# Attention in a fused layer: one exponential over four PSUM banks in place of two over two banks each

## The chip, the core and the metric

The kernel runs on one NeuronCore of a Trainium2 chip, as one program with one launch. The metric is the time of one execution in microseconds on the device. The kernel before takes 879.42 us, the median of 3 runs (879.39 to 880.23).

## What is computed

A transformer layer: grouped-query cross-attention on normalized rows, and then a feed-forward layer with 32 routed experts (8 chosen for each row) and a shared expert. The change lies in the attention.

```python
# x (16, 128, 512), ctx (16, 128, 128); 32 query heads of 16, 8 key/value heads
def attention(q, k, v):
    qh = q.reshape(B, S, KV, G, D).transpose(0, 2, 3, 1, 4)   # KV 8, G 4, D 16
    kh = k.reshape(B, S, KV, D).transpose(0, 2, 1, 3)
    vh = v.reshape(B, S, KV, D).transpose(0, 2, 1, 3)
    scores = einsum('bkgsd,bktd->bkgst', qh, kh) / sqrt(D)
    weights = softmax(scores, axis=-1)
    out = einsum('bkgst,bktd->bkgsd', weights, vh)
    return out.transpose(0, 3, 1, 2, 4).reshape(B, S, E)

x = x + attention(layernorm(x), ctx, ctx)
x = x + moe(layernorm(x))     # gate, 8 of 32 experts, a shared expert
```

## The kernel before

The work is in three stages: attention (up to about 103 us), an end of attention with the last gate logits, the routing and the shared expert (its last shared matmuls start at 210.7 us), and the routed experts (the rest). All engines but the DMA queues of SP run in an order that the source writes out by hand (`manual_schedule`): an engine works through its instructions in the order in which the code issues them, and waits where a semaphore has not come.

**The steps.** `attention_small` makes 32 steps, two for each of the 16 batch elements: in step n, `items[n]` is (b, i), and i picks every other key/value head. The loop at L650 issues, in step n and in this order:

- `head` work: masking of keys (`keys`, L373, on ScalarE, in steps 4, 5, 9, 11, 17 and 19), squares of keys (`squares`, L394, ScalarE, steps 21, 23, 25 and 27), and work for VectorE and GpSimd;
- `scores` of step n (L484): four matmuls (L489), one for each of four key/value heads, each on its own 32 rows of the array (a row tile), each to its own PSUM bank of 128 x 512 float32. Each float32 matmul stands in the trace as two passes, so a step has eight records. Then the exponentials on ScalarE (L499), which read PSUM and write the probabilities `p` to SBUF;
- `values` of step n-1 (L502): four matmuls (L505), which read the probabilities and write one bank, `oT`; VectorE copies it to SBUF as `oTs` (L514);
- in steps 16, 20, 24 and 28 (and 31, after the loop) `gate_parts` (L563), four matmuls (L566) and a copy by ScalarE (L575);
- `transposes` (L447) of one or two sets into the tile `x` of two banks: queries of a later step, normalized rows for the gate, and the attention output of step n-2. ScalarE copies queries as `qT` (L480) and rows as `xall` (L543); VectorE divides the output by the sums (L523, L525), and GpSimd adds it to `x` (L532);
- in steps 17, 21, 25 and 29 `gate_sums` (L577), and then `tail` work, mostly statistics on VectorE.

**PSUM.** There are eight banks. `ps_sc` has two buffers of two banks for the scores, `ps_x` one of two banks, `ps_lg` and `ps_oT` one bank each: eight in all. In `scores`, matmuls 0 and 1 go to the first tile of `ps_sc` and 2 and 3 to the second; each tile has its exponential. The next step's first pair waits for this step's first exponential, and its second pair for the second. The probabilities of a step lie in two tiles of `pp`, which has five buffers.

**The end of attention (L683 to L721).** The scores' banks are used again: `two`, a pair of banks for transposes, and `gu`, a pair for the gate and up sums of the shared expert. `filler(n)` issues the next n matmuls of the shared expert (L282) between other work: the first one after step 31's transposes, the second after the gate parts of rows 8 and 9. The turn of the rows of batch element 15 takes a new pair from `ps_sc` (L714). The last logits let routing begin on ScalarE (L1151) and VectorE (L1159).

Of the kernel before, what the change touches and what calls it, by code (L numbers as in the profile page):

```python
# [9 lines left out]
F32 = mybir.dt.float32  # L10
F16 = mybir.dt.float16
I32 = mybir.dt.int32
AF = mybir.ActivationFunctionType
ALU = mybir.AluOpType
AX = mybir.AxisListType
PSUM = bass.MemoryType.PSUM
DRAM = bass.MemoryType.DRAM

P = 128
EPS = 1e-5  # L20
HD = 16
# [25 lines left out]
def tile_xattn_moe(  # L47
# [15 lines left out]
    nc = tc.nc  # L63
    B, S, D = x.shape
    E, _, ND, I = w1.shape
# [4 lines left out]
    TB = 512  # L70
# [160 lines left out]
    def gate_rows(b, eng):  # L231
        xn = xnp.tile([P, D], F32, tag="xn2", name="xn2", bufs=4)
        normalized(xn, xs[b], b, SECOND, eng)
        nc.sync.dma_start(rows[ts(b, P), 0:D], xn)
        xn2[b] = xn
# [62 lines left out]
    NJ = KV // 2  # L298
    quarter = [slice(4 * k, 4 * k + 4) for k in range(NTB)]

    def attention_small():


        with ExitStack() as ph:
            kpool = ph.enter_context(tc.tile_pool(name="kp", bufs=1))
            ap2 = ph.enter_context(tc.tile_pool(name="ap2", bufs=2))
            pp = ph.enter_context(tc.tile_pool(name="pp", bufs=5))
            ps_sc = ph.enter_context(tc.tile_pool(name="ps_sc", bufs=2, space=PSUM))
            ps_x = ph.enter_context(tc.tile_pool(name="ps_x", bufs=1, space=PSUM))
            ps_lg = ph.enter_context(tc.tile_pool(name="ps_lg", bufs=1, space=PSUM))  # L310
            ps_oT = ph.enter_context(tc.tile_pool(name="ps_oT", bufs=1, space=PSUM))
            qTs, ps, oTs, xqs = {}, {}, {}, {}
# [127 lines left out]
            halves = [slice(h * H, (h + 1) * H) for h in range(2)]  # L440

            def bank_pair(pool):
                return pool.tile(
                    [P, 2, 2, 2, P], F32, tag=("x" if pool is ps_x else "sc"), name="x"
                )

            def transposes(*sets, x=None, between=()):  # L447

                x = bank_pair(ps_x) if x is None else x
                for s, (of, split, _) in enumerate(sets):  # L450
                    for k in range(4):
                        for h, rows in enumerate(halves):
                            if split:
                                to = x[:, h, :, s, ts(k, P // 4)]
                                by = ident[rows, rows].rearrange("p (a b) -> p a b", a=2)
                            else:
                                to = x[:, h, k // 2, s, ts(k % 2, H)]
                                by = ident[rows, rows]
                            nc.tensor.matmul(  # L459
                                to,  # L460
                                lhsT=of[rows, k, :],
                                rhs=by,
                                start=True,
                                stop=True,
                                is_transpose=True,
                                tile_position=(h * H, 0),
                            )
                for s, (_, _, then) in enumerate(sets):
                    if s == len(sets) - 1:
                        for f, a in between:  # L470
                            f(*a)
                    then(x[:, :, :, s])
# [9 lines left out]
                return xn, False, then  # L482

            def scores(b, i):  # L484
                scs = [ps_sc.tile([P, 2, TB], F32, tag="sc", name="sc") for _ in range(NJ // 2)]
                qT = qTs[b].rearrange("p h r s -> p (h r s)")
                for j in range(NJ):
                    rows = slice(j * HP, (j + 1) * HP)
                    nc.tensor.matmul(  # L489
                        scs[j // 2][:, j % 2],  # L490
                        lhsT=kzs[b // 4 % 2][rows, b % 4, i, :],
                        rhs=qT[rows],
                        start=True,
                        stop=True,
                        tile_position=(j * HP, 0),
                    )
                for j, sc in enumerate(scs):
                    p = pp.tile([P, 2, TB], F32, tag="p", name="p")
                    nc.scalar.activation(p, sc, AF.Exp, scale=1.0 / HD**0.5)  # L499
                    ps[b, i, 2 * j], ps[b, i, 2 * j + 1] = p[:, 0], p[:, 1]  # L500

            def values(b, i):  # L502
                oT = ps_oT.tile([P, TB], F32, tag="oT", name="oT")
# [37 lines left out]
            def turn_of(b, copy=nc.scalar.copy):  # L541
                def then(x):
                    copy(  # L543
                        xnT[b // 4][:, :, ts(b % 4, P)].rearrange(
                            "p (r k) (h s) -> p h r k s", r=2, h=2
                        ),
                        x.rearrange("p h r (k s) -> p h r k s", k=2),
                    )

                return xn2.pop(b).rearrange("p (k d) -> p k d", d=P), False, then  # L550
# [99 lines left out]
            for n in range(N):  # L650
                for f, a in head.get(n, ()):
                    f(*a)

                scores(*items[n])
                if n == 1:
                    transposes(queries(1))
                if n > 0:
                    values(*items[n - 1])
                if n in parts and n < N - 1:
                    gate_parts(parts[n])  # L660
                sets = []
                if n % 2 == 0 and 0 < n // 2 < B - 1:
                    sets.append(queries(n // 2 + 1))
                if n in turned:
                    sets.append(turn_of(turned[n]))
                if n > 1:
                    sets.append(added(*items[n - 2], nc.gpsimd if n < N - 1 else nc.vector))
                if n == N - 1:
                    sets.reverse()
                between = middle.get(n, ())  # L670
                if sets:
                    transposes(*sets, between=between)
                else:
                    assert not between
                keep_warm(FILL.get(n, 0))
                if n in sums:
                    gate_sums(sums[n])
                for f, a in tail.get(n, ()):
                    f(*a)
# [2 lines left out]

            gate_rows(12, nc.gpsimd)  # L683
            nc.scalar.activation(table, table, AF.Sigmoid)
            two = bank_pair(ps_sc)
            gu = ps_sc.tile([P, 2, TB], F32, tag="sc", name="gu")
            banks = iter([gu[:, i] for i in range(2)])
            later, products = [], []
            matmuls = shared_up(0, 0, lambda: next(banks), later, products)

# [20 lines left out]
            filler(1)  # L711
            gate_parts(12)
            gate_rows(15, nc.vector)
            transposes(turn_of(15), x=bank_pair(ps_sc))  # L714
            gate_rows(14, nc.vector)
            transposes(turn_of(14, nc.vector.tensor_copy))
            gate_sums(12, nc.scalar.copy)
# [1199 lines left out]

    pieces = [(k, i) for k in range(NTB) for i in range(NI)]
    left_over = attention_small()
    experts(pieces[1:], in_order, *left_over)  # L1920
    left = nc.values_load(
# [64 lines left out]
```

## Time and profile before

The profile is of one execution on the chip. Its own time is 881.58 us, its span (first to last instruction) 879.7 us; the median of the runs is 879.42 us.

| What | Value |
|---|---|
| time of the profiled execution / its span | 881.58 / 879.7 us |
| TensorE matmuls busy | 861.7 us (98% of the span) |
| ScalarE, VectorE, GpSimd busy | 689.4, 625.9, 476.4 us |
| exponentials (L499), 64 of 128 x 1024 | 62.1 us, 1023 ns each |
| score matmul records (L489), 256 | 44.2 us, 639 ns each |
| value matmul records (L505), 256 | 34.1 us, 605 ns each |
| ScalarE idle before exponentials, ended by scores | 13.6 us, 23 times |

A line of a timeline gives the start in us from the start of the span, the duration in us, the engine, the line of the source, the operation, output and input tiles with their shape, and how many instructions are merged in it; in brackets stands the idle time of the engine before it and what ended it. "PE" is TensorE's matmul and "PEld" its loading of weights, which can run beside it. Records of matmuls on different row tiles overlap, so busy time is not a measure of how full the array is. A line of a group gives its busy time and the mean of one instruction, and after the second bar the idle time before it and what ended that. The chain of waits follows the work that ended last back to what released it.

Busy time of the engines by stage (us; the steps' first half, second half, the end of attention, and the beginning of routing):

| Stretch | length | PE | DVE | ACT | POOL |
|---|---|---|---|---|---|
| 8.8 to 55.5 | 46.70 | 46.27 | 39.16 | 37.91 | 24.43 |
| 55.5 to 102.8 | 47.30 | 47.30 | 34.59 | 41.04 | 31.73 |
| 102.8 to 120.2 | 17.40 | 15.86 | 11.05 | 8.93 | 8.29 |
| 120.2 to 160.0 | 39.80 | 39.80 | 34.73 | 11.72 | 9.04 |

### The profile page before, as it was taken

How to read it: one execution, taken by the hardware profiler on the slowest of the kernel's cores; microseconds unless marked ns; L12 is line 12 of the kernel's file. 1: busy time of each engine (PE TensorE's matmuls, PEld its weight loads, DVE VectorE, ACT ScalarE, POOL GpSimd, SP SyncE). 2: the span in 40 equal slices, each digit the busy share in tenths (PEclk: the TensorE clock that was granted, in tenths of full speed). 3: DMA queues.
4: the chain of work that ended last, by engine and by line, in shares of the span. 5: the costliest groups of instructions: out<-in, count | busy, mean ns of one | idle time of the engine just before them, and what ended most of it. 6: DMA issues, size and time to landing. Idle time of an engine off the chain costs nothing.

```text
span 879.7 us, 13628 instructions
## 1 busy us (share of the span) xinstructions
PE 861.7 (98%) x4015; PEld 538.5 (61%) x4015; DVE 625.9 (71%) x1599; ACT 689.4 (78%) x1570; POOL 476.4 (54%) x590
## 2 busy tenths in 40 slices
PE   8999999999899999999999999999999999999995
PEld 5344444546565665666666666676767777777763
DVE  7877778846976777777777777776867777777510
ACT  5888732537998898888898989898898899999831
POOL 4487550053355576656556666565556656554454
PEclk9999999999999999999999999999999999999999
DMA  9111112556377788778778787877778888786544
GB/s 307 58 48 50 49 50 77 211 156 197 110 169 162 172 202 191 177 169 182 165 181 184 192 188 191 186 210 175 187 158 206 195 176 178 197 190 122 88 76 54
DMA packets 59876, 137.15 MB, mean 156 GB/s; under 512 B 12168, under 2 KB 16392, under 8 KB 59792
## 3 DMA queue, kind: packets, MB, share of 16 engines
q0 software_dynamic: 32032, 69.25, 41.9%
q1 hardware_dynamic: 27680, 66.81, 22.1%
q8 instruction: 34, 0.56, 0.3%
q14 instruction: 50, 0.41, 0.2%
q10 hardware_dynamic: 80, 0.13, 0.0%
HBM read 96.71 MB, written 46.73 MB: 163 GB/s over the span
## 4 chain that ended last, share of the span: by engine, by line
PE 88%; POOL 3%; ACT 3%; issue 2%; DVE 2%; DMA 2%; POOLq 0%; ACTq 0%
PE p L1612 42%; PE y L1749 24%; PE gu L282 6%; PE sc L489 5%; PE oT L505 4%; PE x L459 2%; PE y L1386 2%; POOL out_dram L1721 2%; ACT xall L1506 2%; DMA out_dram<-yw,token 1%; PE tok L1038 1%; DVE x L1396 1%; PE lgT L566 0%; PE lg L581 0%; DVE xall L1506 0%
## 5 line engine op out<-in xcount | busy, mean ns | idle before, releaser
L1506 ACT COPY xall<-blocks 32x256 f32<-32x256 f32 (+10 forms) x1137 | 418.9, 368 | 15.0
L1721 POOL DMA_INDIRECT out_dram<-yw,token x150 | 246.2, 1641 | 212.0 <-ACT yw L1765 79.7
L1749 PE MATMUL y<-wdn,sa 128*128 128x512 f32 (+2 forms) x672 | 259.1, 594 | 0.0
L1460 POOL DMA_INDIRECT xgs<-rows,token x138 | 150.7, 1092 | 134.5 <-DVE token L1050 53.2
L1612 PE MATMUL p<-xall,wup 128*128 128x270 f32 (+27 forms) x720 | 185.6, 394 | 2.0 <-ACT p L1661 2.0
L1612 PEld LDWEIGHTS p<-xall,wup 128*128 128x128 f32 x720 | 136.5, 190 | 46.6 <-issue 16.1
L1749 PEld LDWEIGHTS y<-wdn,sa 128*128 128x128 f32 (+2 forms) x672 | 100.9, 171 | 83.7 <-issue 72.2
L1765 ACT ACTIVATE yw<-y,wt 128x512 f32<-128x512 f32 x138 | 94.7, 686 | 70.6 <-PE y L1749 39.4
L1612 PE MATMUL p<-t,s 128*128 128x270 f32 (+27 forms) x480 | 125.7, 394 | 1.1 <-DVE t L1603 1.1
L1612 PEld LDWEIGHTS p<-t,s 128*128 128x128 f32 x480 | 91.0, 190 | 39.0 <-issue 22.4
L1509 DVE STREAM_TRANSPOSE blocks<-xgs 128x512 f32<-128x512 f32 x138 | 97.5, 706 | 0.2
L1622 DVE TENSOR_TENSOR z<-u,p 128x270 f32<-128x270 f32 (+27 forms) x96 | 48.8, 509 | 68.5 <-PE p L1612 63.3
L499 ACT ACTIVATE p<-sc 128x1024 f32<-128x1024 f32 x64 | 62.1, 1023 | 13.6 <-PE sc L489 13.6
L1612 PE MATMUL p<-t,wup 128*128 128x270 f32 (+27 forms) x240 | 63.8, 396 | 0.7 <-DVE z L1622 0.7
L1612 PE MATMUL p<-xall,s 128*128 128x270 f32 (+27 forms) x240 | 63.6, 396 | 0.5 <-DVE z L1622 0.4
L1612 PEld LDWEIGHTS p<-t,wup 128*128 128x128 f32 x240 | 45.0, 190 | 25.9 <-issue 14.1
L282 PE MATMUL gu<-xall,sup 128*128 128x512 f32 x128 | 59.2, 601 | 0.0
L1622 DVE TENSOR_TENSOR u<-u,p 128x270 f32<-128x270 f32 (+27 forms) x48 | 24.4, 509 | 44.9 <-PE p L1612 36.9
L1612 PEld LDWEIGHTS p<-xall,s 128*128 128x128 f32 x240 | 45.2, 190 | 16.9 <-issue 4.3
L1506 DVE COPY xall<-blocks 32x256 f32<-32x256 f32 (+11 forms) x187 | 51.3, 299 | 3.5
L489 PE MATMUL sc<-qT,kz 32*128 32x512 f32 x256 | 44.2, 639 | 0.5 <-DVE qT L480 0.2
L1603 DVE TENSOR_TENSOR t<-xall,t 128x540 f32<-128x540 f32 (+27 forms) x60 | 43.3, 722 | 0.5
(218 smaller groups left out, 916.2 us busy)
## 6 DMA issues: line engine op xcount, KB each, us to landing
wup<-in_w_dram SPq DMA_DIRECT2D x64, 512.0 KB
wdn<-in_w_dram SPq DMA_DIRECT2D x32, 512.0 KB
rows<-xn SPq DMA_DIRECT2D x16, 256.0 KB
out_dram<-x SPq DMA_DIRECT2D x16, 256.0 KB
x<-in_x_dram SPq DMA_DIRECT2D x15, 256.0 KB
out_dram<-yw,token POOLq DMA_INDIRECT x150
xgs<-rows,token POOLq DMA_INDIRECT x138
cTs<-in_cT_dram SPq DMA_DIRECT2D x4, 256.0 KB
```

Source lines behind the costliest of these rows:

```text
L282: nc.tensor.matmul(acc, lhsT=sup[:, w, d, ts(i, P)], rhs=xnT[k][:, d, :], start=(d == 0), stop=(d == ND - 1),)
L489: nc.tensor.matmul(scs[j // 2][:, j % 2], lhsT=kzs[b // 4 % 2][rows, b % 4, i, :], rhs=qT[rows], start=True, stop=True, tile_position=(j * ...
L499: nc.scalar.activation(p, sc, AF.Exp, scale=1.0 / HD**0.5)
L1460: nc.gpsimd.indirect_dma_start(out=t, out_offset=None, in_=rows[:, :], in_offset=bass.IndirectOffsetOnAxis(ap=token[:, j : j + 1], axis=0) ...
L1506: yield on_ACT, 1 + many, lambda dst=dst, of=of, copy=copy: copy(dst, of)
L1509: nc.vector.transpose(blocks[:, j % NB_BUF, :], xgs[:, j % NG_BUF, 0:D])
L1603: yield lambda o=out_, a=a, b=b: nc.vector.tensor_tensor(o, a, b, ALU.subtract)
L1612: nc.tensor.matmul(acc[:, i, 0:h], lhsT=w[:, i, d, :], rhs=x[:, d, :], start=(first and i == d == 0), stop=(i == outs[-1] and d == 1), ski ...
L1622: soon(lambda: nc.vector.tensor_tensor(out_, a, b, ALU.add))
L1721: ins = nc.gpsimd.indirect_dma_start(out=flat, out_offset=bass.IndirectOffsetOnAxis(ap=token2[:, k - 1 : k] if a else token[0:b, j : j + 1 ...
L1749: nc.tensor.matmul(y[c0:c1, :], lhsT=acts_of[k % NA][:, i, col : col + c1 - c0], rhs=wdn[k % NW][:, i, :], start=(i == 0), stop=(i == NI - 1),
L1765: nc.scalar.activation(yws[j], y, AF.Copy, scale=wt[:, j : j + 1])
```

## The change

The scores of a step go to one tile of four banks, and one exponential of 128 x 2048 reads it. `ps_sc` has one buffer of four banks in place of two of two, so PSUM holds the same eight banks. The probabilities of a step are one tile, and `pp` has three buffers of it in place of five half as large. At the end of attention one four-bank tile, `four`, stands for `two` and `gu`, and the turn of element 15 uses its first half again instead of taking a new pair. The matmuls, their order and all other work stay as they are. In the changed source the exponential stands at L496, the scores at L487, the values at L503 and the transposes at L457.

```diff
-            pp = ph.enter_context(tc.tile_pool(name="pp", bufs=5))
-            ps_sc = ph.enter_context(tc.tile_pool(name="ps_sc", bufs=2, space=PSUM))
+            pp = ph.enter_context(tc.tile_pool(name="pp", bufs=3))
+            ps_sc = ph.enter_context(tc.tile_pool(name="ps_sc", bufs=1, space=PSUM))
...
             def scores(b, i):
-                scs = [ps_sc.tile([P, 2, TB], F32, tag="sc", name="sc") for _ in range(NJ // 2)]
+                sc = ps_sc.tile([P, NJ, TB], F32, tag="sc", name="sc")
                 qT = qTs[b].rearrange("p h r s -> p (h r s)")
                 for j in range(NJ):
                     rows = slice(j * HP, (j + 1) * HP)
                     nc.tensor.matmul(
-                        scs[j // 2][:, j % 2],
+                        sc[:, j],
                         lhsT=kzs[b // 4 % 2][rows, b % 4, i, :],
                         rhs=qT[rows],
                         start=True,
                         stop=True,
                         tile_position=(j * HP, 0),
                     )
-                for j, sc in enumerate(scs):
-                    p = pp.tile([P, 2, TB], F32, tag="p", name="p")
-                    nc.scalar.activation(p, sc, AF.Exp, scale=1.0 / HD**0.5)
-                    ps[b, i, 2 * j], ps[b, i, 2 * j + 1] = p[:, 0], p[:, 1]
+                p = pp.tile([P, NJ, TB], F32, tag="p", name="p")
+                nc.scalar.activation(p, sc, AF.Exp, scale=1.0 / HD**0.5)
+                for j in range(NJ):
+                    ps[b, i, j] = p[:, j]
...
-            two = bank_pair(ps_sc)
-            gu = ps_sc.tile([P, 2, TB], F32, tag="sc", name="gu")
-            banks = iter([gu[:, i] for i in range(2)])
+            four = ps_sc.tile([P, NJ, TB], F32, tag="sc", name="four")
+            two = four[:, 0:2].rearrange("p h (r s t) -> p h r s t", r=2, s=2)
+            banks = iter([four[:, i] for i in (2, 3)])
...
-            transposes(turn_of(15), x=bank_pair(ps_sc))
+            transposes(turn_of(15), x=two)
```

More of the change, by code (lines that the diff above doesn't have):

```diff
@@ L442, in bank_pair @@
             def bank_pair(pool):
-                return pool.tile(
-                    [P, 2, 2, 2, P], F32, tag=("x" if pool is ps_x else "sc"), name="x"
-                )
+                return pool.tile([P, 2, 2, 2, P], F32, tag="x", name="x")
             def transposes(*sets, x=None, between=()):
```

## Prediction

> **What bounds the kernel now.** I read the page first: one core, granted clock at full speed in every slice, and a chain that is TensorE for 88% of the span. The lines of the changed code in it are the scores (L489), the values (L505) and the transposes (L459).
>
> ```profile
> PE 88%; POOL 3%; ACT 3%; issue 2%; DVE 2%; DMA 2%; POOLq 0%; ACTq 0%
> PE p L1612 42%; PE y L1749 24%; PE gu L282 6%; PE sc L489 5%; PE oT L505 4%; PE x L459 2%; PE y L1386 2%; POOL out_dram L1721 2%; ACT xall L1506 2%; DMA out_dram<-yw,token 1%; PE tok L1038 1%; DVE x L1396 1%; PE lgT L566 0%; PE lg L581 0%; DVE xall L1506 0%
> ```
>
> So only the first 103 us matter, where 32 attention steps run; the rest is downstream of them. The timeline of steps 18 and 19 shows the order on TensorE: scores, values of the step before, transposes, sometimes gate work, and the next scores.
>
> ```profile
> 62.38 1.14 PE L489 MATMUL sc<-qT,kz 32*128 32x512 f32 x8
> ...
> 63.45 1.06 PE L505 MATMUL oT<-p,va 128*32 128x512 f32 x8
> 63.62 1.94 ACT L499 ACTIVATE p<-sc 128x1024 f32<-128x1024 f32 x2 [0.85 <-PE sc L489]
> ...
> 64.45 0.46 PE L459 MATMUL x<-ident,xq 64*128 64x64 f32 x8
> ...
> 64.75 0.41 PE L459 MATMUL x<-ident,oTs 64*128 64x64 f32 x8
> 65.09 0.30 PEld L489 LDWEIGHTS sc<-qT,kz 32*128 32x128 f32 x4
> 65.09 1.65 PE L489 MATMUL sc<-qT,kz 32*128 32x512 f32 x8
> ...
> 65.61 0.30 PEld L489 LDWEIGHTS sc<-qT,kz 32*128 32x128 f32 x4 [0.22 <-ACT p L499]
> ...
> 66.67 1.06 PE L505 MATMUL oT<-p,va 128*32 128x512 f32 x8
> ```
>
> Read it as a loop of two engines. Undisturbed scores take TensorE 1.07 us (62.38 to 63.45), values 1.00 (to 64.45), two sets of transposes 0.64 (to 65.09): 2.71 us a step. The exponentials begin 1.24 after the scores' start (63.62) and end at 65.56, 3.18 after it. TensorE is back at 65.09, so step 19 starts its first pair on banks that the first exponential has freed, and its second pair at 65.61, 0.05 after the second exponential. TensorE therefore already waits for ScalarE in many steps, but only with half of its scores: those groups last up to 1.8 us instead of 1.07. Long and short steps alternate (2.71 from 62.38 to 65.09, then 3.22 to 68.31).
>
> **What the Trainium skill says.** (1) "ScalarE: Activation LUTs", *What ACT_TABLE_LOAD costs*: an ACTIVATE with immediate scale and bias takes 186 ns + 0.833 ns an element, and back-to-back ones overlap by about 93 ns. For 1024 elements that is an estimated 1.04 us; the trace has 1.02 (row below), and two take 1.94, an overlap of 0.10. It agrees.
>
> ```profile
> L499 ACT ACTIVATE p<-sc 128x1024 f32<-128x1024 f32 x64 | 62.1, 1023 | 13.6 <-PE sc L489 13.6
> ```
>
> (2) "TensorEngine Tiling (Array Packing)", *Key Properties*: different tiles work in parallel. The trace agrees: four row tiles with two passes each end in 1.07 us, though one pass alone reads 0.6. Hence a late pair costs its whole 1.07 again. (3) "Perfetto Trace Analysis", *Optimizing Scalar/DVE Operations*: larger operations raise throughput if the engine is saturated; where it is not and causes bubbles elsewhere, smaller ones finish sooner. ScalarE is busy 41.0 of 47.3 us in the second half of the steps, 37.9 of 46.7 in the first, so it is the second case. (4) "TensorE: Matmul & The Clock Gate", Part 1: the clock falls after an idle window of about 3.4 us. No stall below is as long; no run here shows a fall.
>
> **The change part by part.**
>
> *One exponential.* 1024 more elements at 0.83 ns are 0.85 us: 1.02 + 0.85 = 1.88 us (by the skill's price 1.89) against 1.94 for the pair. It saves 0.06 a step on ScalarE, 2 us in all if ScalarE alone set the time. Bounds: 1.85, and 1.94 (no saving).
>
> *One tile of four banks instead of two of two.* All eight banks were taken (4 + 2 + 1 + 1), so the pool falls from two buffers to one. In the built program the four score matmuls had two waits for ScalarE (first and third), and now have one, on the first, for the exponential before. Behind it in TensorE's order stand values, gate matmuls, transposes. The exponential in turn needs all four score matmuls. No overlap of scores and exponential is left: a step cannot be shorter than 1.24 (scores' start to exponential's) + 1.88 + 0.05 = 3.17 us. The 0.05 and the behaviour of a first pair that waits are in step 1: its first exponential ends at 11.02, the scores start at 11.07.
>
> What covers this wait is TensorE's own work. A plain step has 2.71 us, or 2.39 with one set of transposes, so 0.46 or more stays open. A step with gate parts is ready after 1.07 + 2.07 = 3.14 (its 2.07 from the values' start to the next scores, as from 69.59 to 71.66): just covered. A step with gate sums takes 3.27 (59.18 to 62.45 in the chain) and stays limited by TensorE.
>
> *What is late next.* ScalarE's other work fits in the 1.29 us while it waits (0.05 + 1.24). A copy occupies about 0.47, key masking 0.61, gate copy 0.26, squares 0.51 (each less 0.12 of overlap). The fullest gap, after step 20, is 0.26 + 0.47 + 0.51 = 1.24, and it starts 0.12 before the exponential's end. VectorE is busy 39.2 of 46.7 us and gets more room. The probabilities, three deep by step, were two and a half deep: no wait.
>
> *Sum.* Step 0 at 8.83, exponential at 10.00, so step 1 at 10.00 + 1.88 + 0.05 = 11.93 (before: 11.07). Step 2 at 11.93 + 1.18 + 1.88 + 0.05 = 15.04 (before: 14.44; 1.18 as from 11.07 to 12.25). Steps 2 to 16: 14 x 3.17 = 44.4, to 59.4 (before: 55.47). Steps 16 to 31: four with gate sums at 3.27 and eleven at 3.17 = 48.0, to 107.4 (before: 102.76). That is +4.6 us.
>
> *The end of attention.* The first shared matmul after the steps needs step 31's exponential and stood 3.02 after its scores (102.76 to 105.78); now 3.17: +0.15. The tail's turned tile and the first shared sums become one four-bank tile, and the built order adds a wait for ScalarE to the second shared matmul: I take it for the copy of the turned tile. That ends at 110.05, the matmul began at 109.76: 110.05 + 0.05 - 109.76 = +0.34. Behind it stand the gate sums of rows 8 and 9 and all later logits. If the wait is another, it costs nothing. The later turn into the same banks has the same wait as before. The removed eviction waits: none.
>
> ```profile
> 109.46 0.59 ACT L543 COPY xall<-x 128x512 f32<-128x512 f32 x1
> ...
> 109.77 1.12 PE L282 MATMUL gu<-xall,sup 128*128 128x512 f32 x2
> ```
>
> Routing starts from the last logits (120.38), the gathers from routing, the experts from the gathers; I see nothing with a start of its own that would absorb the delay. Sum: 4.6 + 0.15 + 0.34 = 5.1 us. Of the profiled execution the span goes from 879.7 to 884.8 and its 881.58 to 886.7; that execution is 2.2 us above the median of the runs, 879.42, to which I add the same 5.1: 884.5 us.
>
> **Rivals.**
>
> *Faster: the ragged starts vanish.* In the chain the score groups above 1.07 us add up to about 7.8 us over the 31 steps. If TensorE found the whole tile free on arrival, all groups would take 1.07, and the time would be 879.4 - 7.8 = 871.6. For it: ScalarE loses a start a step and waits 13.6 us for scores today. Against: TensorE arrives 2.71 after the scores' start, the exponential ends at 3.12. It decides the sign once the exponential takes under 1.42 us (2.71 - 1.24 - 0.05), or TensorE's own work between score groups reaches 2.10 instead of 1.64. Neither is in the trace.
>
> *Slower still: ScalarE's side work gets in the way.* With no second buffer, copies, masks and squares (10 steps have masks or squares) could delay the exponential instead of hiding in the gap; today key masking delays step 19's (1.44 instead of 1.24). At 0.3 in each of 10 steps, 3.0 us more: 887.5. The gap count above speaks against it.
>
> *No change.* The lost 5 us could be taken back if the routing or the first gathers waited for something that does not move. The windows after 103 us show TensorE at work throughout and no long DMA wait: time 879.4.
>
> **How the numbers follow.** Forecast 0.80; ragged starts vanish 0.06; side work in the way 0.09; no change 0.05. Forecast's own range: period 3.11 instead of 3.17 takes 1.6 us off, a free tail wait 0.3: 882.5. An exponential of 1.94 adds 1.6 and the side work up to half of its rival's price 1.5: 887.6. This leaves out less than 2 in 10. About 0.2% (1.8 us) is what a measurement can tell from no change. Slower by more: 0.80 and 0.09, less a little for the lower end: 0.89. Same 0.05, faster 0.06.
>
> **What would show it.** Right: score groups of 1.07 us again, all four starting together about 0.05 after the exponential; steps of 3.17 where long and short alternated; one ACTIVATE of 128x2048 near 1.88 us; step 31 near 107.4; waits of TensorE's loads for the exponential near 0.45 in plain steps; the tail from step 31 to the long run of shared matmuls some 0.5 longer (17.4 before). Wrong: steps of 2.7 us, an exponential far from 1.88, or a stage after routing that shrinks.

## The result and the profile after

The changed kernel takes 886.0 us (median of 6 runs, 885.45 to 886.79), the kernel before takes 879.78 beside it (6 runs, 879.23 to 880.23). The ratio is 1.0071, 95% interval 1.0058 to 1.0084: 6.2 us slower. The profiled execution took 886.2 us with a span of 884.4.

First the page's chain of waits, then the two groups of the changed code (busy time and mean of one; idle time before it and what ended it).

```profile
PE 80%; ACT 7%; POOL 4%; issue 3%; DMA 3%; DVE 2%; POOLq 0%; ACTq 0%; DVEq 0%
...
L496 ACT ACTIVATE p<-sc 128x2048 f32<-128x2048 f32 x32 | 60.2, 1880 | 23.3 <-PE sc L487 23.2
...
L487 PE MATMUL sc<-qT,kz 32*128 32x512 f32 x256 | 36.5, 639 | 12.0 <-ACT p L496 11.8
```

The first line is the chain's shares by engine (the kernel before: PE 88%, ACT 3%). ScalarE's busy time in exponentials fell by 1.9 us (62.1 to 60.2), yet its idle time before them rose from 13.6 to 23.3 us, 23.2 of them waiting for scores. TensorE in turn is idle 11.8 us before scores, waiting for exponentials. So their work on the scores' banks goes by turns, without overlap. The chain followed back from the time of step 31's exponential says so too; first that of the kernel before (8.8 to 105 us), then that of the changed one (8.8 to 110 us):

```profile
by line: PE sc L489 43.9%; PE oT L505 31.0%; PE x L459 18.6%; PE lg L581 2.3%; ACT p L499 2.1%; PE lgT L566 1.8%; issue 0.3%; PE kT L411 0.2%
```

```profile
by line: ACT p L496 44.8%; PE sc L487 36.8%; PE oT L503 7.9%; PE x L457 5.1%; issue 2.8%; PE lg L579 2.2%; PE lgT L564 1.7%; ACTq L496 0.3%
```

The exponential's share went from 2.1% to 44.8%, and that of values and transposes from 49.6% to 13.0%: they now lie beside it. The timeline of steps 19 and 20 of the changed kernel shows the new loop:

```profile
69.84 1.14 PE L487 MATMUL sc<-qT,kz 32*128 32x512 f32 x8 [0.73 <-ACT p L496]
...
70.91 1.06 PE L503 MATMUL oT<-p,va 128*32 128x512 f32 x8
71.11 1.88 ACT L496 ACTIVATE p<-sc 128x2048 f32<-128x2048 f32 x1 [0.23 <-PE sc L487]
71.91 0.46 PE L457 MATMUL x<-ident,xn 64*128 64x64 f32 x8
72.21 0.41 PE L457 MATMUL x<-ident,oTs 64*128 64x64 f32 x8
...
73.04 1.14 PE L487 MATMUL sc<-qT,kz 32*128 32x512 f32 x8 [0.42 <-ACT p L496]
```

The scores start at 69.84 and the exponential at 71.11 (1.27 later); it ends at 72.99, and the next scores start at 73.04, 0.05 after it. The step is 3.20 us long. TensorE has been idle for 0.42 by then, with its other work of the step all done. The table follows the delay through the profiled executions (us).

| Start of | before | after | difference |
|---|---|---|---|
| scores of step 2 | 14.44 | 15.11 | 0.67 |
| scores of step 16 | 55.47 | 59.86 | 4.39 |
| scores of step 31 | 102.76 | 108.34 | 5.58 |
| first shared matmul after the steps | 105.78 | 111.54 | 5.76 |
| second | 109.76 | 115.86 | 6.10 |
| routing (sigmoid of the last logits) | 120.63 | 126.71 | 6.08 |
| routed experts, first matmul of L1612 (L1610 after) | 224.93 | 231.01 | 6.08 |

From routing to that matmul of the routed experts the difference stays 6.08. After that the two profiled executions come closer, to 4.6 us at the end, and this wants a reason: the kernel before lost 1.1 us of these 1.5 in one place, at 226 us, waiting for VectorE. An execution of the kernel before that was profiled once more (`before_again` below) had no such wait. So the shrinking after 226 us is an accident of one execution, and the change costs the 6.1 us of the trace, as the medians say (6.2).

### The profile page after: what moved, and what is told of

The parts are those of the page before. It is cut to its first block, busy times and chain, and to the rows that moved or that the text cites. A ratio compares the mean times of both kernels' runs of the same rounds, so it can differ in the third digit from the quotient of the medians.

```text
span 884.4 us, 13567 instructions
## 1 busy us (share of the span) xinstructions
PE 856.1 (97%) x4015; PEld 534.8 (60%) x4015; DVE 627.5 (71%) x1599; ACT 686.9 (78%) x1538; POOL 480.0 (54%) x590
## 4 chain that ended last, share of the span: by engine, by line
PE 80%; ACT 7%; POOL 4%; issue 3%; DMA 3%; DVE 2%; POOLq 0%; ACTq 0%; DVEq 0%
PE p L1610 40%; PE y L1747 23%; PE gu L282 6%; ACT p L496 5%; PE sc L487 4%; POOL out_dram L1719 3%; DMA out_dram<-yw,token 3%; PE y L1384 3%; ACT xall L1504 2%; PE oT L503 1%; PE tok L1036 1%; PE four L282 1%; PE x L457 1%; PE lg L579 0%; DVE x L1394 0%
## 5 line engine op out<-in xcount | busy, mean ns | idle before, releaser
L1458 POOL DMA_INDIRECT xgs<-rows,token x138 | 154.5, 1119 | 131.6 <-DVE token L1048 53.2
L1610 PE MATMUL p<-xall,wup 128*128 128x270 f32 (+27 forms) x720 | 185.6, 394 | 1.9 <-ACT p L1659 1.9
L1610 PEld LDWEIGHTS p<-xall,wup 128*128 128x128 f32 x720 | 136.5, 190 | 46.5 <-issue 16.1
L1610 PE MATMUL p<-t,s 128*128 128x270 f32 (+27 forms) x480 | 125.6, 394 | 0.0
L1610 PEld LDWEIGHTS p<-t,s 128*128 128x128 f32 x480 | 91.1, 190 | 37.6 <-issue 22.4
L496 ACT ACTIVATE p<-sc 128x2048 f32<-128x2048 f32 x32 | 60.2, 1880 | 23.3 <-PE sc L487 23.2
L1610 PE MATMUL p<-t,wup 128*128 128x270 f32 (+27 forms) x240 | 63.8, 396 | 0.7 <-DVE z L1620 0.7
L1610 PE MATMUL p<-xall,s 128*128 128x270 f32 (+27 forms) x240 | 63.6, 396 | 0.5 <-DVE z L1620 0.4
L1610 PEld LDWEIGHTS p<-t,wup 128*128 128x128 f32 x240 | 45.0, 190 | 25.9 <-issue 14.3
L1610 PEld LDWEIGHTS p<-xall,s 128*128 128x128 f32 x240 | 45.2, 190 | 16.9 <-issue 3.7
L282 PE MATMUL gu<-xall,sup 128*128 128x512 f32 x112 | 51.0, 598 | 0.0
L487 PE MATMUL sc<-qT,kz 32*128 32x512 f32 x256 | 36.5, 639 | 12.0 <-ACT p L496 11.8
```

The lines of the kernel that those rows point to most:

```text
L282: nc.tensor.matmul(acc, lhsT=sup[:, w, d, ts(i, P)], rhs=xnT[k][:, d, :], start=(d == 0), stop=(d == ND - 1),)
L487: nc.tensor.matmul(sc[:, j], lhsT=kzs[b // 4 % 2][rows, b % 4, i, :], rhs=qT[rows], start=True, stop=True, tile_position=(j * HP, 0),)
L1458: nc.gpsimd.indirect_dma_start(out=t, out_offset=None, in_=rows[:, :], in_offset=bass.IndirectOffsetOnAxis(ap=token[:, j : j + 1], axis=0) ...
L1610: nc.tensor.matmul(acc[:, i, 0:h], lhsT=w[:, i, d, :], rhs=x[:, d, :], start=(first and i == d == 0), stop=(i == outs[-1] and d == 1), ski ...
```

## The experiments

Theory: a single buffer of four banks makes scores and exponential of a step exclude each other, so that a step lasts as long as the way round (scores, exponential, scores). Rivals: the longer instruction itself is the cost; ScalarE's side work delays it; TensorE is slowed in some other way; and part of the loss is at the end of attention or hidden by the luck of one execution. Ratios are to the kernel before in runs on the same chip. The chips differ by up to 3 us (medians of the kernel before from 877.58 to 880.57), so absolute times of runs on different chips aren't compared.

### The buffer kept, the instruction cut in two (`one_tile_two_exp`)

```diff
-                nc.scalar.activation(p, sc, AF.Exp, scale=1.0 / HD**0.5)
+                for h in range(2):
+                    pair = slice(2 * h, 2 * h + 2)
+                    nc.scalar.activation(p[:, pair], sc[:, pair], AF.Exp, scale=1.0 / HD**0.5)
```

> The changed kernel, with the one exponential of a step cut into two of 128x1024 again, on the same single four-bank tile. Theory (the single buffer is what costs: scores and exponentials of neighbouring steps can no longer overlap): the loss stays and grows a little, since two exponentials take 1.94 us where one takes 1.88: steps of 1.27 + 1.94 + 0.05 = 3.26 us instead of 3.20, about 887.5 us in all. Rival (the longer instruction costs, by handing over its result and its banks later): near 880 again.

Measured: 888.1 us against 880.57, ratio 1.0085 (1.0068 to 1.0102), 7.5 us slower. The timeline of steps 6 and 7:

```profile
28.20 1.14 PE L487 MATMUL sc<-qT,kz 32*128 32x512 f32 x8 [0.73 <-ACT p L498]
...
29.46 1.94 ACT L498 ACTIVATE p<-sc 128x1024 f32<-128x1024 f32 x2 [1.32 <-PE sc L487]
...
31.46 1.14 PE L487 MATMUL sc<-qT,kz 32*128 32x512 f32 x8 [0.49 <-ACT p L498]
```

Two short exponentials on one buffer wait just as one long one does, and need 1.94 instead of 1.88 us. The first of them, alone, is this record:

```profile
29.46 1.02 ACT L498 ACTIVATE p<-sc 128x1024 f32<-128x1024 f32 x1 [1.32 <-PE sc L487]
```

It has read two of the four banks by 30.48, yet the next scores into these banks start with the others at 31.46, 0.05 after the second exponential's end. So what they wait for is the whole tile, and cutting the instruction frees nothing. The step is 3.26 instead of 3.20 long, the scores of step 31 start at 109.95 instead of 108.34. The long instruction is not the loss; it is the part of the change that helps, by 0.06 us a step. The rival falls. (The total is a weaker witness: in the profiled execution the granted clock was 0.5 for 3.4 us at 241.8 us.)

### The end of attention with two tiles again (`tail_two_tiles`, `tail_two_pools`)

The steps as in the changed kernel; before the end the pool of the step's banks is closed, and new tiles take its place: in the first kernel two from one pool, in the second one each from two pools.

```diff
...
-            four = ps_sc.tile([P, NJ, TB], F32, tag="sc", name="four")
-            two = four[:, 0:2].rearrange("p h (r s t) -> p h r s t", r=2, s=2)
-            banks = iter([four[:, i] for i in (2, 3)])
+            step_banks.close()
+            ps_end = ph.enter_context(tc.tile_pool(name="ps_end", bufs=2, space=PSUM))
+            two = bank_pair(ps_end)
+            gu = ps_end.tile([P, 2, TB], F32, tag="x", name="gu")
+            banks = iter([gu[:, i] for i in range(2)])
```

In `tail_two_pools` the last lines are instead:

```diff
+            ps_gate = ph.enter_context(tc.tile_pool(name="ps_gate", bufs=1, space=PSUM))
+            ps_two = ph.enter_context(tc.tile_pool(name="ps_two", bufs=1, space=PSUM))
+            gu = ps_gate.tile([P, 2, TB], F32, tag="x", name="gu")
+            two = bank_pair(ps_two)
```

> The changed kernel, with only the end of attention as before: after step 31 the score banks are given back and taken again as two tiles of two banks. Theory (the second shared matmul waits for the copy of the turned rows because both lie in one tile): the second shared matmul starts 0.34 us earlier, so that from the scores of step 31 to the long run of shared matmuls it is 17.55 us instead of 17.9; the steps are unchanged at 3.20. Rival (that wait belongs to something else): 17.9 as in the changed kernel.

Measured: 893.83 us against 880.57, ratio 1.0152 (1.0131 to 1.0173). The second shared matmul did come 0.33 earlier (7.19 us after the scores of step 31 instead of 7.52), and routing 0.32 earlier, but some 7.5 us were lost after that (13.3 in all, 5.8 of them there at routing). The wait, and the windows from there on (length, busy time of PE, PEld, DVE, ACT and POOL with numbers of instructions, granted clock, DMA share, GB/s):

```profile
PEld gu L282 <- DVE sa L293: 4.8, 1, 4.8
```

```profile
118.00:126.00 8.00, 7.03 (x67) 3.83 (x67) 2.99 (x11) 3.02 (x9) 0.90 (x1) 1.00 0.27 100
126.00:131.00 5.00, 4.29 (x6) 1.40 (x5) 3.98 (x10) 2.70 (x4) 4.86 (x36) 0.66 0.01 2
131.00:140.00 9.00, 5.88 (x7) 2.52 (x8) 5.54 (x8) 0.00 (x0) 4.18 (x106) 0.62 0.00 1
```

Two things meet here that are no part of the change. The next stage's sums got a wait of 4.8 us for a product that reads the old `gu`; I take it that the pool's two tiles come free together. And the granted clock fell to half twice, for 3.4 us at 126.1 and for 6.8 us at 133.0. So this run shows the 0.33 us and nothing on the total. Hence the second form:

> The changed kernel with the end of attention in two tiles again, this time from two pools of their own, so that the first shared sums of the routing stage no longer wait for the product of the last ones (which cost 4.8 us in the run with one pool, together with two stretches of half clock). Theory: second shared matmul 0.33 us earlier than in the changed kernel, steps unchanged at 3.20, and nothing lost after it: 885.7 us on a chip where the kernel before takes 879.8, a loss of 5.8 us. Rival (two tiles at the end cost more than they save): 6.5 us of loss or more.

Measured: 883.19 us against 877.79, ratio 1.0058 (1.0043 to 1.0073), 5.4 us slower. Its timeline at the end of attention, and after it that of the changed kernel:

```profile
115.17 0.59 ACT L542 COPY xall<-x 128x512 f32<-128x512 f32 x1 [0.68 <-DVE at L524]
...
115.39 1.12 PE L282 MATMUL gu<-xall,sup 128*128 128x512 f32 x2
```

```profile
115.22 0.59 ACT L541 COPY xall<-four 128x512 f32<-128x512 f32 x1 [0.58 <-DVE at L523]
...
115.86 1.12 PE L282 MATMUL four<-xall,sup 128*128 128x512 f32 x2 [0.26 <-ACT xall L541]
```

With two tiles the shared matmul starts inside the copy; with one it starts 0.05 after the copy's end, though copy and matmul use different banks. The dependency goes by tile. Routing starts 18.04 us after the scores of step 31 instead of 18.37, and the token matmuls at 157.14 instead of 157.60. Of these 0.46 us, 0.14 stood there at step 31 already (108.20 instead of 108.34). The shared tile thus accounts for 0.3 us of the loss, the end of attention as a whole for 0.5 (5.58 to 6.08 in the table above), the steps for the rest. (That the total lost 5.4 and not the 5.8 of the expectation lies within its interval.) Neither the wait of 4.8 us nor the half clock came back. The second form has two pools and also takes the pair for the sums before the other one; which of the two removes the wait isn't separated.

### Smaller pieces instead of larger (`five_banks`, `five_banks_pools`)

Five score tiles of one bank each, four exponentials of 128 x 512 in a step. The fifth bank is the gate's, which joins the rotation, so scores have one bank more than in the other kernels. The probabilities have ten buffers of a bank's size, two and a half steps as in the kernel before. The end is that of `tail_two_tiles` and of `tail_two_pools`.

```diff
...
-                sc = ps_sc.tile([P, NJ, TB], F32, tag="sc", name="sc")
+                scs = [ps_sc.tile([P, TB], F32, tag="sc", name="sc") for _ in range(NJ)]
...
-                        sc[:, j],
+                        scs[j],
...
-                p = pp.tile([P, NJ, TB], F32, tag="p", name="p")
-                nc.scalar.activation(p, sc, AF.Exp, scale=1.0 / HD**0.5)
-                for j in range(NJ):
-                    ps[b, i, j] = p[:, j]
+                for j, sc in enumerate(scs):
+                    p = pp.tile([P, TB], F32, tag="p", name="p")
+                    nc.scalar.activation(p, sc, AF.Exp, scale=1.0 / HD**0.5)
+                    ps[b, i, j] = p
...
```

> The other direction: scores in five tiles of one bank each (the gate's bank joins the rotation), with four exponentials of 128x512 a step, the end of attention as before the change. Theory (what counts is how early the last score matmul of the next step gets its bank): the last row tile waits for the third exponential instead of the last, at 1.25 + 2 x 0.49 + 0.60 + 0.05 = 2.88 us after the scores' start. Steps of about 2.9 where the kernel before had 2.96 on average and the changed one 3.20; step 31 starts near 100.3; about 877.5 us. Rival (ScalarE's number of instructions sets the step): 128 instead of 32 exponentials add 0.2 us a step, 886 us or more.

Measured: 886.67 us against 880.57, ratio 1.0069 (1.0051 to 1.0087). The steps did what was expected: the scores of step 31 start at 100.65, 2.1 us before those of the kernel before, and routing at 118.86 instead of 120.63. Then some 8 us went the same way as above: a wait of the same kind (4.7 us), and half clock at 118.4, 125.2 and 241.3. The total misses the expectation and stands where the rival had it, but for a reason that lies outside the steps.

> Five score tiles of one bank with four exponentials a step, the end of attention in two tiles from two pools of their own. In the run with one pool step 31 started at 100.65 us and routing at 118.9 (kernel before: 102.8 and 120.6), and the gain was lost after that to the same wait and to half clock. Theory: step 31 at 100.7, routing at 118.7 to 118.9, and the gain stays: 1.8 us below the kernel before. Rival (the finer tiles lose it again after routing has begun): no faster than the kernel before.

Measured: 875.72 us against 877.79, ratio 0.9973 (0.9963 to 0.9983): 2.1 us faster than the kernel before, and the fastest of all kernels here. The timeline of steps 26 to 28, first here and then in the kernel before:

```profile
85.40 1.14 PE L493 MATMUL sc<-qT,kz 32*128 32x512 f32 x8
86.47 1.06 PE L509 MATMUL oT<-p,va 128*32 128x512 f32 x8
86.56 2.07 ACT L503 ACTIVATE p<-sc 128x512 f32<-128x512 f32 x4 [0.72 <-PE sc L493]
...
88.11 1.20 PE L493 MATMUL sc<-qT,kz 32*128 32x512 f32 x8
...
90.88 1.38 PE L493 MATMUL sc<-qT,kz 32*128 32x512 f32 x8
```

```profile
87.39 1.14 PE L489 MATMUL sc<-qT,kz 32*128 32x512 f32 x8
...
90.09 1.65 PE L489 MATMUL sc<-qT,kz 32*128 32x512 f32 x8
...
93.31 1.26 PE L489 MATMUL sc<-qT,kz 32*128 32x512 f32 x8
```

Step 26 takes 2.71 us in both, TensorE's own work. The gain is in step 27, 2.77 instead of 3.22 us: its scores take 1.20 us where the late second pair of the kernel before makes them 1.65. Over steps 2 to 31 the mean is 2.96 instead of 3.05. ScalarE is busier meanwhile: 2.07 us for its four pieces, more than the 1.94 of the kernel before and the 1.88 of the changed one. But its first piece starts 1.16 after the scores' start, and by 88.11 it has freed banks.

"Perfetto Trace Analysis", *Optimizing Scalar/DVE Operations*, of the Trainium skill says that where an engine is not saturated but makes others wait, breaking up its instructions may let work finish sooner. The runs agree, under a condition that they add: four pieces with a tile each bring 2.1 us, two pieces on one tile (`one_tile_two_exp`) cost 0.06 us a step. How much of the 2.1 us is due to the fifth bank is not shown, since no run has four tiles of one bank.

### Is it the exponential's time that sets the step? (`half_exp`)

The exponential reads only the first half of each bank, and the values read its probabilities twice; half of the probabilities are left out.

```diff
-                p = pp.tile([P, NJ, TB], F32, tag="p", name="p")
-                nc.scalar.activation(p, sc, AF.Exp, scale=1.0 / HD**0.5)
+                p = pp.tile([P, NJ, TB // 2], F32, tag="p", name="p")
+                nc.scalar.activation(p, sc[:, :, 0 : TB // 2], AF.Exp, scale=1.0 / HD**0.5)
...
-                        rhs=ps.pop((b, i, j)),
+                        rhs=ps.pop((b, i, j)).unsqueeze(1).to_broadcast([P, 2, TB // 2]),
```

> The changed kernel with an exponential over the first half of the columns of each bank (128x1024 in all); the values' matmuls read these twice, so half of the probabilities is left out, and routing sees other rows. Read the steps, not the total. Theory: the wait for the exponential ends 1.27 + 1.02 + 0.05 = 2.34 us after the scores' start, below TensorE's own 2.4 to 2.7, so TensorE sets the step: scores without waits for ScalarE, steps of 2.71 (2.39 with one set of transposes), step 31 near 96. Rival (VectorE or another chain holds the steps at about 3 us anyway): step 31 at 102 or later.

Measured: the whole took 3581 us in its one run, which I put down to other routing (the kernel has a second path for unbalanced experts, which was not examined), so only the steps are read. Their groups:

```profile
L496 ACT ACTIVATE p<-sc 128x1024 f32<-128x1024 f32 x32 | 32.8, 1024 | 21.3 <-PE sc L487 21.2
...
L487 PE MATMUL sc<-qT,kz 32*128 32x512 f32 x256 | 36.5, 639 | 0.6 <-ACT p L496 0.4 <-DVE qT L478 0.2
```

TensorE's wait for exponentials went from 11.8 to 0.4 us (second line), and step 31 starts at 98.38, before 102.76 and far before 108.34. With the exponential at 1.02 us the one buffer costs nothing, since 1.27 + 1.02 + 0.05 = 2.34 lies under TensorE's 2.71. But 98.38 is 2.4 later than I expected. The second half runs at TensorE's own pace, 44.8 us from step 16 to 31; the first averages 2.83 a step, and there another wait came up, five times and 2.1 us in all:

```profile
27.68 0.46 PE L457 MATMUL x<-ident,xq 64*128 64x64 f32 x8 [0.28 <-DVE at L523]
...
33.41 0.46 PE L457 MATMUL x<-ident,xq 64*128 64x64 f32 x8 [0.38 <-DVE at L523]
```

The transposes wait for VectorE's division, which frees their banks. My expectation had left VectorE out as the next bound.

### TensorE's idle time filled (`again_after`, `again_before`)

In steps 2 to 15 the first set of transposes is issued twice, in the changed kernel and in the kernel before.

```diff
-            def transposes(*sets, x=None, between=()):
+            def transposes(*sets, x=None, between=(), again=False):
...
-                    for k in range(4):
+                    for k in [*range(4)] * (2 if again and s == 0 else 1):
...
-                    transposes(*sets, between=between)
+                    transposes(*sets, between=between, again=2 <= n <= 15)
```

> The changed kernel with the first set of transposes of steps 2 to 15 issued twice (8 more matmuls, 0.25 us of TensorE a step, same result). Theory (TensorE has at least 0.46 us to spare in each of these steps while it waits for the exponential): nothing is lost, step 16 starts at 59.9 as in the changed kernel, 886.0 us. Rival (TensorE's own work sets the steps): 14 x 0.25 = 3.5 us more.

> The same added transposes in the kernel before. Theory (there TensorE and the pairs of exponentials set the steps in turn: two neighbouring steps take 2.96 + 3.22 instead of 2.71 + 3.21): about 0.13 us a step, 1.8 us in all, step 16 near 57.3. Rival (the waits swallow it here too): no change.

Measured, on one chip: `again_after` 883.89 us against 877.58, ratio 1.0077 (1.0061 to 1.0094), 6.3 us slower where the changed kernel alone was 6.2 slower. `again_before` 879.15 us, ratio 1.0017 (1.0010 to 1.0024), 1.6 us slower. The timeline of the first, where the doubled transposes stand as x16:

```profile
28.13 1.14 PE L487 MATMUL sc<-qT,kz 32*128 32x512 f32 x8 [0.43 <-ACT p L496]
...
30.20 0.72 PE L457 MATMUL x<-ident,xq 64*128 64x64 f32 x16
30.75 0.42 PE L457 MATMUL x<-ident,oTs 64*128 64x64 f32 x8
31.33 1.14 PE L487 MATMUL sc<-qT,kz 32*128 32x512 f32 x8 [0.17 <-ACT p L496]
```

The extra work shortens the two waits shown to 0.43 and 0.17 us, from 0.67 and 0.42 at the same places of the changed kernel, and leaves the step at 3.20; steps 2 to 16 take 44.74 us (44.75 without it). In the kernel before the same work shifts step 16 by 1.9 us (57.46 after a step 2 at 14.52). Each doubled set is 0.25 us, 3.5 in 14 steps. All of it is free in the changed kernel, and 1.9 us of it lie on the path in the kernel before, whose steps TensorE and the exponentials limit by turns: the bound has moved from TensorE to the way round.

### The kernel before once more (`before_again`)

No edit.

> The kernel before once more, for its profile. Its first profiled execution lost 1.1 us on TensorE at 226 us, waiting for VectorE at the first routed expert, which the changed kernel's did not. Theory (chance of one execution, the change's true cost is the 6.1 us that stood at 222 us): no such wait, span near 877.9. Rival (the kernel before always has it, and the change gives 1.5 us back there): the wait is there again, span near 879.7.

Measured: 877.87 us, ratio 1.0002 (0.9993 to 1.0011). Steps and routing start as in the first profile (step 31 at 102.78, routing at 120.63). Below, at 226 us, first the first execution and then this one:

```profile
227.36 2.63 PE L1612 MATMUL p<-t,s 128*128 128x352 f32 x8 [1.09 <-DVE t L1603]
```

```profile
226.11 2.53 PE L1612 MATMUL p<-t,s 128*128 128x352 f32 x8
```

The wait is missing in the second. That the change gives something back among the experts is therefore not borne out.

## Why the prediction was right, step by step

The forecast was 884.5 us, 5.1 more than before; measured are 886.0 and 6.2 more. The mechanism was right, and one term was too small. (Of the 1.5 us between 884.5 and 886.0, 0.4 is the kernel before, which measured 879.78 beside it instead of 879.42.) No error made up for another.

- *One exponential, 1.88 us, saving 0.06.* Right: 1.880, and 0.06 a step is what cutting it in two costs again (3.20 to 3.26).
- *One buffer ends the overlap.* Right: all score groups have 1.07 us (0.55 to the last pass's start). All four matmuls start together, and 0.05 after the exponential's end except after gate sums. Half an exponential, the added transposes and, less purely, five banks each show it from another side.
- *The length of the way round, 3.17.* This is the term that was mis-sized. It measured 1.27 + 1.88 + 0.05 = 3.20. I had taken the 1.24 from the scores' start to the exponential's from the kernel before, where the exponential waits for the first pair only; one that waits for the whole tile starts 0.03 later, also where it reads only half of the tile (`one_tile_two_exp`). By step 16 this made 0.44 us (59.86 for 59.42), and 0.22 after it.
- *The remaining 0.31 us* is step 18: its exponential starts 1.58 instead of 1.27 after the scores (below). Together 0.97 us, from the prediction's 107.37 for step 31, rounded to 107.4 there, to 108.34: nearly all that the forecast missed of the change.
- *Steps with gate sums 3.27.* Right, TensorE-bound as before. Steps with gate parts: I said ready after 3.14 and just covered; they took 3.20, as long as the longer way round. Steps of 3.14 came elsewhere (1, 2, 23 and 27): there the exponential starts 1.21 after the scores. Why is open.
- *ScalarE's side work fits into the gap.* Right but for the unexplained step 18, in which no mask and no squares stand. The rival that added 3.0 us for it didn't come; that 886.0 lies halfway to its 887.5 has the two other reasons above.
- *End of attention, 0.15 + 0.34.* Measured 0.18 + 0.33 (5.58, 5.76 and 6.10 in the table). The second wait was indeed for the copy of the turned tile, shown by the two forms with separate tiles.
- *Nothing downstream absorbs it.* Right: 6.08 at routing and among the routed experts.
- *Of the rivals*, the ragged starts vanished as named, but by waiting for the whole tile and not by finding it free: the exponential needed 1.88 and the point from which it decides was 1.42. `half_exp`, below that point at 1.02, shows the other side.
- *"No run here shows a fall" of the clock* was wrong even of the one trace that I had, as the last section shows. The forecast doesn't rest on it. Of the ragged score groups, "up to 1.8 us" leaves out step 1, whose group lasts 1.97.

## What to carry to other kernels

Before merging instructions to save their start cost, count the buffers: if the merged tile takes all the banks of its pool, producer and consumer exclude each other, and the step is the sum of their times and both handovers (here 1.27 + 1.88 + 0.05) instead of the longer of the two. Time saved on an engine that waits for its input need not show: here 1.9 us less of exponentials came with 6.2 us more in all. Smaller tiles that free banks earlier can gain even though the engine gets busier (2.07 us of exponentials in a step, and 2.1 us faster, with a fifth bank). Look also at what a tile ties together: here a shared tile cost 0.33 us between work on different banks.

## What the runs showed of the hardware beside that

*Half clock.* "TensorE: Matmul & The Clock Gate", Part 1, of the Trainium skill has the clock fall after an idle window of about 3.4 us. The prediction said that no run showed a fall. The trace of the kernel before has one, at 875.4 us, 5.2 us after the end of TensorE's last matmul, and so has the end of every other trace here. One fall in a later run fits too, at 870.2 in `half_exp`, 4.3 us into a gap of 10.2 us of TensorE. Two lie within gaps of 3.8 to 3.9 us, at 133.0 in `tail_two_tiles` and at 125.2 in `five_banks`, but only 2.7 and 2.3 us after the gap's start. The others had no such gap. At 126.1 in `tail_two_tiles` TensorE was busy in 7.03 of the 8 us before (the changed kernel, 7.04 of 8, didn't fall); 118.4 in `five_banks`, 122.1 in `again_before` and 115.9 in `half_exp` stand at the same place of the program, just before routing. At 241.3 in `five_banks` and 241.8 in `one_tile_two_exp` a gap of 1.97 us stands before, which the first trace of the kernel before has too, ending at 234.9, without a fall. These last 3.4 us; at 126.1 a matmul of 512 columns is recorded every 0.85 us instead of 0.43. So a gap of 3.4 us was not needed here, and what decides which execution falls stays open.

*A late exponential.* In step 18 the exponential of the changed kernel starts 0.31 us late, with ScalarE idle and the scores' records ended:

```profile
66.33 1.14 PE L487 MATMUL sc<-qT,kz 32*128 32x512 f32 x8
```

```profile
67.91 1.88 ACT L496 ACTIVATE p<-sc 128x2048 f32<-128x2048 f32 x1 [1.22 <-PE sc L487]
```

It is the same step in `tail_two_tiles`, `tail_two_pools`, `again_after` and `half_exp`, and step 14 in `one_tile_two_exp`, which has more instructions ahead of it. In all six runs an instruction fetch of 8 KB starts 0.6 to 0.7 us after it (68.59 here, 56.50 in `one_tile_two_exp`), but another such fetch, at 91.54 here, has no late exponential beside it. That the instruction supply is the cause is a guess; no run tested it.
